# Attention and feed-forward block on one Trainium2 core: weight counting moved to the feed-forward, copies of the large products moved to ScalarE, side work held back at a unit's end

## Chip, core and metric

The kernel runs on one NeuronCore of a Trainium2 chip. The metric is the device time of one execution in microseconds (us), the median of several runs. One further execution was taken by the hardware profiler; all durations of single instructions below come from that one.

The engines go by these names: PE is TensorE's matrix multiply and PEld its weight load, DVE is VectorE, ACT is ScalarE, POOL is GpSimd, SP is SyncE, which here only issues transfers. [...]

## The reference

A transformer block in float32 for 4 sequences of 1024 tokens of 256 numbers, with 16 heads of 16 numbers, and a gated feed-forward network with 1024 hidden numbers and ternary weights:

```python
# x: (4, 1024, 256)
x = x + layernorm(attention(layernorm(x), Wqkv, Wout))
x = x + layernorm(ffn(layernorm(x), w1, w2, h1, h2, w3))

def attention(x, Wqkv, Wout):              # per head
    e = exp(clip(scores - max, -50, 50))
    attn = e / (sum(e) + 1e-6)             # out = (attn @ v) @ Wout.T

def ffn(x, ...):
    h = silu(x @ w1.T * w1_s) * (x @ w2.T * w2_s)
    h = gelu(h @ h1.T * h1_s)
    h = gelu(h @ h2.T * h2_s)
    return h @ w3.T * w3_s
```

## The kernel before

`tile_fast` computes the whole block under two assumptions: the scores are small enough to do without subtracting the maximum, and the feed-forward weights are exactly representable in the reduced type fp32r, so that one rounded copy of each weight does for an exact product. Both are tested on the chip. A column of the tile `misses` receives, for each piece of weight, the number of entries at which the weight and its rounded copy differ; two further columns per sequence tell of the scores. `judge` sums them, the sum goes into `bad`, and where `bad` is above zero `tile_general` computes all again. It isn't entered here.

**Attention.** A unit is one sequence `b`, one group `g` of 4 heads and one half `h` of the queries; there are 4 x 4 x 2 = 32 units. Each unit has 8 key chunks `c` and 2 head pairs `u`, so 16 tiles, 512 in all. For each tile `exponentials` issues 2 matmuls of scores `s` (L461) and one Exp activation `e<-s` of 128 x 1024 (L462) on ACT; `weigh` issues 4 matmuls per tile that add `e` times the values into `acc` (L469). The scores lie in the three PSUM buffers `ps`, the exponentials in a ring of 8 tiles, and `acc` has one buffer. `rise` keeps a running maximum `top` of the exponentials on DVE (L478). At the end of a unit `unit_end` copies `acc` to `o` on DVE (L275), and `divide` transposes `top` and `o` on PE into a `ps` buffer `po` (L488, L490) and divides on DVE.

**Side work.** All else is cut into small steps and put into chains of the class `Side`: the normalization of the next sequence (`gather`, `root`, `apply`), its transposes `pt`, its projections `p` (to q and k, `project`) and `pv` (to v, `values`), the ending of a finished half (transposes `po` at L516, output projection `py`, normalization, residual), the checks of the scores, and the rounding and counting of the weights. The main loop runs in turns. In a turn it issues 3 tiles of scores and exponentials, weighs 2 or 4 tiles, and calls `side.take()`, which runs the steps that are due: each step has a gap, the number of turns since the step before it in its chain, and at most one step of a turn uses PE. Side products on PE all use one PSUM buffer, `misc`; it comes free when the copy out of it has read it. The copies are made by one of two helpers:

```python
def to_scalar(o, i, scale=1.0):
    nc.scalar.activation(o, i, AF.Copy, scale=scale)
def to_vector(o, i, scale=1.0):
    nc.vector.tensor_scalar(o, i, scale, None, ALU.mult)
```

In the start-up of sequence 0 (`alone`) the copies run on ACT; later ones run on DVE (L275), except those of the last ending, which run on ACT (L272). `project` needs the product twice: `hi` is the copy in fp32r, and `lo`, made on DVE (L335), the product less `hi`.

**Weights.** `check_weights` treats 22 blocks of 128 x 1024 in one chain: a transfer on POOL's queue loads a block into `w` (L248, one buffer), POOL casts it into `wr` (L252, one buffer), DVE compares in two halves of 128 x 512 (`count`, L258, 44 in all), and after the second half POOL's queue writes `wr` to device memory (L260). Near the end of attention SP's queue loads these rounded weights into buffers that attention no longer needs.

**Feed-forward.** 8 units of 512 tokens. `gated` computes the gated layer into `ha` in 8 steps of 8 matmuls `pg` (L749), with Silu (L763) and a cast (L753) on ACT and two operations on DVE (L765, L754). `gelu_layer` runs twice, in 4 steps of 2 x 16 matmuls `ph` (L749), with Gelu on ACT (L785), a cast and a subtraction on DVE (L786, L787). `finish` computes `pz` (L802). `gated` calls `side.take()` 4 times in a unit (8 times in unit 0), each `gelu_layer` 16 times, and `side.flush()` runs what is left ahead of `finish`. The side work here is the normalization before (`prepare`) and after (`finish`) and the output stores on SP's queue.

Of the kernel before, what the change touches and what calls it, by code (L numbers as in the profile page):

```python
# [9 lines left out]
F32 = mybir.dt.float32  # L10
# [4 lines left out]
ALU = mybir.AluOpType  # L15
# [3 lines left out]
P = 128  # L19
# [16 lines left out]
NQ = 512  # L36
WIDE = 1024
# [78 lines left out]
def tile_fast(ctx: ExitStack, tc: tile.TileContext, x, wqk, wv, wo, w1, w1s, w2, w2s, h1, h1s, h2, h2s, w3, w3s, out, bad):  # L116
    nc = tc.nc
    B, S, D = x.shape
    HID = w1.shape[1]
    DC = D // P  # L120
    HC = HID // P
    NT = S // P
# [10 lines left out]
    xs = [xpool.tile([P, NT, D], F32, tag=f"x{b}", name=f"x{b}") for b in range(B)]  # L133
# [26 lines left out]
    weights = {"w1": w1, "w2": w2, "w3": w3, "h1": h1, "h2": h2}  # L160
    rows_at_once = {n: WIDE // w.shape[1] for n, w in weights.items()}
    blocks = [(n, c) for n, w in weights.items() for c in range(0, w.shape[0] // P, rows_at_once[n])]
    counts = len(blocks) * (WIDE // NQ)
    misses = const.tile([P, counts + B * 2], F32, name="misses")
    nc.vector.memset(misses, 0.0)
    rounded = {n: dram.tile(list(w.shape), F32R, name=f"{n}_r") for n, w in weights.items()}
# [11 lines left out]
    with ExitStack() as actx, ExitStack() as rctx:  # L178
# [56 lines left out]
        def misc(name):  # L235
            return ps_misc.tile([P, NQ], F32, tag="misc", name=name)

        def check_weights(n, c):

            k = blocks.index((n, c))  # L240
            st = {}

            def rows(w):
                return w[c * P : (c + rows_at_once[n]) * P, :].rearrange("(i p) d -> p i d", p=P)

            def load():
                st["w"] = work.tile([P, WIDE], F32, tag="w", name="w", bufs=1)
                nc.gpsimd.dma_start(out=st["w"].rearrange("p (i d) -> p i d", i=rows_at_once[n]), in_=rows(weights[n]))  # L248

            def cast():  # L250
                st["r"] = work.tile([P, WIDE], F32R, tag="wr", name="wr", bufs=1)
                nc.gpsimd.tensor_copy(st["r"], st["w"])  # L252

            def count(j):
                def run():
                    w, r = (t[:, NQ * j : NQ * (j + 1)] for t in (st["w"], st["r"]))
                    i = k * (WIDE // NQ) + j
                    nc.vector.scalar_tensor_tensor(w, w, 1.0, r.bitcast(F32), ALU.mult, ALU.not_equal, accum_out=misses[:, i : i + 1])  # L258
                    if NQ * (j + 1) == WIDE:
                        nc.gpsimd.dma_start(out=rows(rounded[n]).bitcast(F32), in_=st["r"].bitcast(F32).rearrange("p (i d) -> p i d", i=rows_at_once[n]))  # L260

                return run

            return [Step(load, 0, False), Step(cast, 3, False)] + [Step(count(j), 1, False) for j in range(WIDE // NQ)]

        def by_slots(o, w, i, **flags):

# [3 lines left out]
        def to_scalar(o, i, scale=1.0):  # L271
            nc.scalar.activation(o, i, AF.Copy, scale=scale)  # L272
# [4 lines left out]
        def prologue(b, space, copy):  # L277
# [38 lines left out]
            def values(t0):  # L316
                def run():
                    pv = space(f"pv_{b}_{t0}").rearrange("p (t d) -> p t d", d=D)
                    for i in range(2):
                        for c in range(DC):  # L320
                            by_slots(pv[:, i, :], st["xT"][:, c, (t0 + i) * P : (t0 + i + 1) * P], wv_sb[:, c, :], start=c == 0, stop=c == DC - 1)
                    copy(cv[:, t0 : t0 + 2, :], pv)

                return run

            def project(w, m, h):
                def run():
                    pp = space(f"p{w}_{b}_{m}_{h}")
                    for c in range(DC):
                        heads = wqk_sb[:, c, w, HPT * m : HPT * (m + 1), :].rearrange("p h d -> p (h d)")  # L330
                        by_slots(pp, heads, st["xT"][:, c, h * NQ : (h + 1) * NQ], start=c == 0, stop=c == DC - 1)
                    hi, lo = (cq[w, m, k][:, h * NQ : (h + 1) * NQ] for k in ("hi", "lo"))
                    scale = 1.0 if w else 1.0 / math.sqrt(DH)
                    copy(hi, pp, scale)
                    nc.vector.scalar_tensor_tensor(lo, pp, scale, hi.bitcast(F32), ALU.mult, ALU.subtract)  # L335

                return run
# [167 lines left out]
        def ending(b, h, copy):  # L505

            st = {}

            def transposes(c):
                def run():  # L510
                    if c == 0:
                        st["oT"] = work.tile([P, DC, NQ], F32, tag="oT", name=f"oT_{b}_{h}", bufs=1)
                        st["y"] = (both if h else work).tile([P, TPQ, D], F32, tag="y", name=f"y_{b}_{h}", bufs=1)
                    pt = misc(f"po_{b}_{h}_{c}")
                    for t in range(TPQ):
                        nc.tensor.transpose(pt[:, t * P : (t + 1) * P], on[h][:, t, c * P : (c + 1) * P], ident)  # L516
                    copy(st["oT"][:, c, :], pt)

                return run

            def project(t0):
                def run():
                    py = misc(f"py_{b}_{h}_{t0}").rearrange("p (t d) -> p t d", d=D)
                    for i in range(2):
                        for c in range(DC):
                            by_slots(py[:, i, :], st["oT"][:, c, (t0 + i) * P : (t0 + i + 1) * P], wo_sb[:, c, :], start=c == 0, stop=c == DC - 1)
                    copy(st["y"][:, t0 : t0 + 2, :], py)

                return run

            def gather(i):
                def run():
                    st["mv"] = norms.gather([st["y"][:, j, :] for j in range(i, i + 2)], i, st.get("mv"))

                return run

            def root():
                st["ln"] = norms.root(st["mv"])

            def apply(i0):  # L540
                def run():
                    for i in range(i0, i0 + 2):
                        norms.apply(st["y"][:, i, :], st["y"][:, i, :], st["ln"], i)

                return run

            def residual(i):
                def run():
                    xr = xs[b][:, h * TPQ + i : h * TPQ + i + 2, :]
                    nc.vector.tensor_add(xr, xr, st["y"][:, i : i + 2, :])  # L550

                return run

            return (
                [Step(transposes(c), 1) for c in range(DC)] + [Step(project(t), 2 if t else 1, heavy=True) for t in range(0, TPQ, 2)]
                + ([Step(open_ffn, 0, False)] if (b, h) == (B - 1, NH - 1) else [])
                + [Step(gather(i), 1, False) for i in range(0, TPQ, 2)] + [Step(root, 0, False)]
                + [Step(apply(i), 1, False) for i in range(0, TPQ, 2)] + [Step(residual(i), 1, False) for i in range(0, TPQ, 2)]
            )

        class Side:
# [27 lines left out]
                        steps.pop(0)  # L589
                return False  # L590

            def take(self):

                self.slot += 1
                self.borrowed = False
                free, heavy = True, False
                for chain in self.first + self.rest:
                    while step := self.due(chain, self.slot, free):
                        chain[0].pop(0)
                        chain[1] = self.slot  # L600
                        step.run()
                        free = free and not step.tensor
                        heavy = heavy or step.heavy
                self.tired = heavy
# [184 lines left out]
        def finish(n, i):  # L789
# [47 lines left out]
                + [Step(apply(i), 1, False) for i in range(0, TPQ, 2)] + [Step(add(t), 1, False) for t in range(0, TPQ, 2)] + [Step(store, 0, False)]  # L837
            )

        def judge():  # L840

            st = {}

            def add():
                st["total"] = small.tile([P, 1], F32, tag="total", name="total")
                nc.vector.tensor_reduce(st["total"], misses, AX.X, ALU.add)

            def run():
                pn = misc("pn")
                nc.tensor.matmul(pn[0:1, 0:1], st["total"], ones, start=True, stop=True)  # L850
                nc.vector.tensor_copy(bad, pn[0:1, 0:1])

            return [Step(add, 0, False), Step(run, 4)]

        def feed_forward():

            chain = ends[B - 1, NH - 1]
            for n in range(len(halves_of)):

                gated(ffn["a"], 2 if n else 1)  # L860
                if n + 1 < len(halves_of):
                    chain[0].extend(prepare(n + 1, to_scalar))
                if n == 1:
                    side.add(judge())
                gelu_layer(ffn["b"], ffn["a"], "h1")
                gelu_layer(ffn["a"], ffn["b"], "h2")
                side.flush()
                chain = side.add(finish(n, ffn["a"]), True)
            side.flush()
# [36 lines left out]
        early = [v[1], Step(slots(0, 0, 0, NT // 2), 0, False)]  # L906
        side.add(early + v[2:] + [Step(slots(0, 0), 0, False), Step(slots(0, 1), 0, False)] + sum(qk[1], []) + [Step(lambda: later.update(qk1=0, v=0), 0, False), Step(lambda: side.add(flags[0] + flags[1]), 0, False)])
        begin(0)
        side.add([s for k in blocks for s in check_weights(*k)])
        made = seen = weighed = 0  # L910

        def make(end):
# [6 lines left out]
        while weighed < len(tiles):  # L919
# [20 lines left out]
                        break  # L940
            make(end)
            if weighed < len(tiles):
                side.take()

        load_weights("h1", range(HC // 2, HC))
        rctx.close()
# [238 lines left out]
```

## Time and profile before

| | |
|---|---|
| median of 3 runs | 1327.92 us (1327.89 to 1328.0) |
| profiled execution, own time | 1327.01 us |
| its span | 1324.8 us |
| mean granted TensorE clock | 0.993 |
| attention with its start-up | about 0 to 650 us of the span |
| feed-forward | about 650 to 1324.8 us |
| instructions: PE, DVE, ACT, POOL | 8194, 1573, 847, 166 |

The span is the time from the first to the last instruction of the profiled execution; the 2.2 us by which its own time is longer lie around it. The busy share of an engine over the span mixes the two stages, which have different limits, so the stages are read apart. Matmul ends are modelled in the trace[...]; time in which PE waits is read from the list of waits and from the chain of work that ended last.

### The profile page before, as it was taken

To read this page: it belongs to the slowest core of one execution; us is meant where nothing else is said; L and a number is where in the kernel's file an instruction comes from. 1 tells how busy PE (TensorE), PEld (TensorE's weight loads), DVE (VectorE), ACT (ScalarE), POOL (GpSimd) and SP (SyncE) were. 2 spreads that over 40 slices of the span, in tenths; PEclk is the share of its full clock that TensorE was granted. 3 is DMA by queue.
4 is the path that set the end of the run, shared out by engine and by line. 5 is a ranking of instruction groups with operands and counts; after the bars stand their busy time and mean duration, and the time that the engine had idled before them with its cause. 6 is when DMAs were issued, how large, how long until landed. Compare 5 with 4: busy or idle time off the path is not lost.

```text
span 1324.8 us, 21087 instructions
## 1 busy us (share of the span) xinstructions
PE 1263.9 (95%) x8194; PEld 776.6 (59%) x8194; DVE 729.9 (55%) x1573; ACT 697.5 (53%) x847; POOL 119.6 (9%) x166
## 2 busy tenths in 40 slices
PE   7889998999989999989999999999999999999995
PEld 3333333333333334333578888888888888888885
DVE  3576668766696556646573543636436263463533
ACT  3688876887778878988631422414123141231410
POOL 6211112111121000000000000000000000000000
PEclk8999999999999999999999999999999999999998
DMA  4675443554444333334220000000000000000000
GB/s 130 154 188 123 107 103 97 122 116 118 104 99 118 75 65 65 56 64 167 81 112 0 1 16 1 17 0 11 6 1 17 0 17 1 0 17 0 17 0 20
DMA packets 38670, 79.76 MB, mean 60 GB/s; under 512 B 11296, under 2 KB 21152, under 8 KB 38560
## 3 DMA queue, kind: packets, MB, share of 16 engines
q1 hardware_dynamic: 30672, 53.66, 18.5%
q0 software_dynamic: 7360, 24.12, 5.6%
q8 instruction: 67, 1.10, 0.4%
q10 hardware_dynamic: 528, 0.52, 0.2%
q14 instruction: 43, 0.35, 0.1%
HBM read 28.98 MB, written 15.73 MB: 34 GB/s over the span
## 4 chain that ended last, share of the span: by engine, by line
PE 78%; DVE 11%; ACT 5%; issue 2%; DMA 2%; SPq 1%; POOL 0%; ACTq 0%; POOLq 0%; DVEq 0%
PE ph L749 35%; PE acc L469 13%; PE s L461 9%; PE pg L749 5%; PE pz L802 4%; ACT e L462 4%; PE p L269 4%; PE py L269 2%; PE pv L269 2%; DVE top L478 2%; DVE sg L765 1%; PE po L490 1%; DVE st L94 1%; DVE o L275 1%; DVE ha_lo L754 1%
## 5 line engine op out<-in xcount | busy, mean ns | idle before, releaser
L462 ACT ACTIVATE e<-s 128x1024 f32<-128x1024 f32 x512 | 485.5, 1032 | 121.2 <-PE s L461 107.3
L469 PE MATMUL acc<-e,vaug 128*32 128x512 f32 x2048 | 255.1, 600 | 1.6 <-POOL vaug L439 1.6
L785 ACT ACTIVATE a<-ph,h_scale 128x512 f32<-128x512 f32 x128 | 81.0, 685 | 306.2 <-PE ph L749 306.2
L461 PE MATMUL s<-sq,sk 64*128 64x512 f32 x1024 | 192.3, 450 | 13.9 <-ACT e L462 11.4
L749 PE MATMUL ph<-hb_lo,h 128*128 128x512 f32 x512 | 199.4, 389 | 0.0
L749 PE MATMUL ph<-hb_hi,h 128*128 128x512 f32 x512 | 199.4, 389 | 0.0
L461 PEld LDWEIGHTS s<-sq,sk 64*128 64x128 f32 x1024 | 86.0, 185 | 153.4 <-ACT e L462 119.8
L478 DVE TENSOR_TENSOR top<-top,e 128x512 f32<-128x512 f32 x192 | 135.6, 706 | 29.6 <-ACT e L462 23.4
L786 DVE CAST ha_hi<-a 128x512 fp32r<-128x512 f32 x64 | 27.1, 424 | 158.2 <-ACT a L785 158.2
L469 PEld LDWEIGHTS acc<-e,vaug 128*32 128x32 f32 x2048 | 49.2, 108 | 107.0 <-issue 98.0
L104 POOL TENSOR_TENSOR rstd<-ve,minus_half 128x4 f32<-128x4 f32 (+1 forms) x33 | 37.1, 1125 | 799.0 <-DVE ve L102 799.0
L749 PEld LDWEIGHTS ph<-hb_lo,h 128*128 128x128 f32 x512 | 96.1, 188 | 20.1
L749 PEld LDWEIGHTS ph<-hb_hi,h 128*128 128x128 f32 x512 | 96.1, 188 | 20.1
L749 PE MATMUL ph<-ha_hi,sq 128*128 128x512 f32 x256 | 101.9, 398 | 0.4
L749 PE MATMUL ph<-ha_lo,sq 128*128 128x512 f32 x256 | 99.8, 390 | 0.0
L749 PE MATMUL ph<-ha_lo,sk 128*128 128x512 f32 x256 | 99.7, 390 | 0.0
L749 PE MATMUL ph<-ha_hi,sk 128*128 128x512 f32 x256 | 99.7, 389 | 0.0
L765 DVE SCALAR_TENSOR_TENSOR sg<-pg,w_scale,sg 128x512 f32<-128x512 f32 x64 | 47.1, 745 | 48.1 <-ACT sg L763 48.1
L763 ACT ACTIVATE sg<-pg,w_scale 128x512 f32<-128x512 f32 x64 | 43.3, 688 | 55.1 <-DVE ha_lo L754 44.3
L786 DVE CAST hb_hi<-a 128x512 fp32r<-128x512 f32 x64 | 27.0, 422 | 80.4 <-ACT a L785 80.4
L269 PE MATMUL p<-xT,wqk_sb 128*32 128x512 f32 x512 | 61.6, 602 | 2.0 <-DVE xT L275 1.1
L749 PEld LDWEIGHTS ph<-ha_hi,sq 128*128 128x128 f32 x256 | 48.3, 189 | 12.8 <-DVE sg L765 3.4
(145 smaller groups left out, 1649.7 us busy)
## 6 DMA issues: line engine op xcount, KB each, us to landing
w<-in_h_dram POOLq DMA_DIRECT2D x16, 512.0 KB, 4.7
h_r<-wr POOLq DMA_DIRECT2D x16, 512.0 KB, 3.4
sk<-ck1hi SPq DMA_DIRECT2D x64, 64.0 KB, 2.3
sk<-ck1lo SPq DMA_DIRECT2D x64, 64.0 KB, 2.3
sq<-cq1hi SPq DMA_DIRECT2D x64, 64.0 KB, 2.3
sq<-cq1lo SPq DMA_DIRECT2D x64, 64.0 KB, 2.3
h<-h_r SPq DMA_DIRECT2D x8, 512.0 KB, 6.4
sk<-ck0hi SPq DMA_DIRECT2D x56, 64.0 KB, 2.3
```

The source lines that it names most:

```text
L104: nc.gpsimd.tensor_tensor(rstd[:, :n], ve[:, :n], self.minus_half[:, :n], ALU.pow)
L269: nc.tensor.matmul(o[j : j + SLOT, :], w[:, j : j + SLOT], i, **flags)
L461: nc.tensor.matmul(s[:, a, :], stacks[1, g % 2, u][r, c * P : (c + 1) * P], stacks[0, g % 2, u][r, h * NQ : (h + 1) * NQ], start=True, sto ...
L462: nc.scalar.activation(pair(k)[:, u], s, AF.Exp)
L469: nc.tensor.matmul(acc[SLOT * i : SLOT * (i + 1), :], vaug[g % 2][:, c, i, :], pair(k)[:, i // 2, i % 2, :], start=c == 0, stop=c == NT - 1)
L478: nc.vector.tensor_max(top, top if c > 1 else pair(k - 2)[:, :, :, 0:P], pair(k)[:, :, :, 0:P])
L749: nc.tensor.matmul(p, homes[n][c][:, m * P : (m + 1) * P], half[:, c, :], start=c == 0 and k == 0, stop=c == len(homes[n]) - 1 and k == 1)
L763: nc.scalar.activation(sg, p[:, 0, :], AF.Silu, scale=scales["w1"][:, m : m + 1])
L765: nc.vector.scalar_tensor_tensor(sg, p[:, 1, :], scales["w2"][:, m : m + 1], sg, ALU.mult, ALU.mult)
L785: nc.scalar.activation(a, p[:, j, :], AF.Gelu, scale=scales[n][:, m : m + 1])
L786: nc.vector.tensor_copy(o[0][:, m, :], a)
L802: nc.tensor.matmul(p[t], half[:, c, t * P : (t + 1) * P], homes["w3"][c], start=c == 0 and k == 0, stop=c == HC - 1 and k == 1)
```

## The change

Three edits.

- Rounding and counting are parted. In attention `round_weights` loads, casts and writes each block with no step on DVE. In the feed-forward a new `check_weights` makes 44 pieces of 128 x 512. For each, SP's queue loads the weight again into one of two slots in the buffer of sequence 0 (`xs[0]`, whose first half is free from unit 2 on), and DVE compares it with the rounded copy that lies in on-chip memory. Units 2 to 6 take 9, 9, 9, 9 and 8 pieces, queued after `gated` and ahead of the two `gelu_layer`s; `judge` follows in unit 6 instead of unit 1.
- `values`, `project` and, except for the last sequence, the output projection `py` copy their products with `to_scalar` wherever they run. `xT`, `oT` and `o` stay on DVE, and so do the subtractions for `lo`.
- `Side.take` has a flag `calm`. With it set, steps that don't use PE wait for a later turn. It is set when no more than 4 tiles of the current unit are left to weigh (or no more than are made and not yet weighed, if that is fewer).

```diff
-    counts = len(blocks) * (WIDE // NQ)
+    counts = sum(w.shape[0] * w.shape[1] for w in weights.values()) // (P * NQ)
...
-        def check_weights(n, c):
-            k = blocks.index((n, c))
+        def round_weights(n, c):
...
             def cast():
                 st["r"] = work.tile([P, WIDE], F32R, tag="wr", name="wr", bufs=1)
                 nc.gpsimd.tensor_copy(st["r"], st["w"])
-            def count(j):
-                def run():
-                    w, r = (t[:, NQ * j : NQ * (j + 1)] for t in (st["w"], st["r"]))
-                    i = k * (WIDE // NQ) + j
-                    nc.vector.scalar_tensor_tensor(w, w, 1.0, r.bitcast(F32), ALU.mult, ALU.not_equal, accum_out=misses[:, i : i + 1])
-                    if NQ * (j + 1) == WIDE:
-                        nc.gpsimd.dma_start(out=rows(rounded[n]).bitcast(F32), in_=...)
-                return run
-            return [Step(load, 0, False), Step(cast, 3, False)] + [Step(count(j), 1, False) for j in range(WIDE // NQ)]
+                nc.gpsimd.dma_start(out=rows(rounded[n]).bitcast(F32), in_=...)
+            return [Step(load, 1, False), Step(cast, 3, False)]
...
-                    copy(cv[:, t0 : t0 + 2, :], pv)
+                    to_scalar(cv[:, t0 : t0 + 2, :], pv)
...
-                    copy(hi, pp, scale)
+                    to_scalar(hi, pp, scale)
                     nc.vector.scalar_tensor_tensor(lo, pp, scale, hi.bitcast(F32), ALU.mult, ALU.subtract)
...
-                    copy(st["y"][:, t0 : t0 + 2, :], py)
+                    (copy if b == B - 1 else to_scalar)(st["y"][:, t0 : t0 + 2, :], py)
...
-            def take(self):
+            def take(self, calm=False):
...
-                    while step := self.due(chain, self.slot, free):
+                    while (step := self.due(chain, self.slot, free)) and (step.tensor or not calm):
...
+        def check_weights():
+            parts = []
+            for n, w in weights.items():
...
+                        parts.append(count(len(parts), w[...].rearrange("(i p) d -> p i d", p=P), n, c, j))
+            return parts
+        def count(k, rows, n, c, j):
+            st = {}
+            def load():
+                st["w"] = xs[0][:, 2 * (k % 2) : 2 * (k % 2) + 2, :].rearrange("p t d -> p (t d)")
+                nc.sync.dma_start(out=st["w"].rearrange("p (i d) -> p i d", i=rows.shape[1]), in_=rows)
+            def run():
+                r = spare[6 + c // (HC // 2)][:, D * c % WIDE :][:, :NQ] if n == "w3" else homes[n][c][:, j : j + NQ]
+                nc.vector.scalar_tensor_tensor(st["w"], st["w"], 1.0, r.bitcast(F32), ALU.mult, ALU.not_equal, accum_out=misses[:, k : k + 1])
+            return [Step(load, 1, False), Step(run, 2, False)]
...
             for n in range(len(halves_of)):
                 gated(ffn["a"], 2 if n else 1)
...
-                if n == 1:
-                    side.add(judge())
+                if 1 < n < len(halves_of) - 1:
+                    size = -(-len(checks) // (len(halves_of) - 3))
+                    side.add(sum(checks[size * (n - 2) : size * (n - 1)], []) + (judge() if n == len(halves_of) - 2 else []))
...
-        side.add([s for k in blocks for s in check_weights(*k)])
+        side.add([s for k in blocks for s in round_weights(*k)])
...
-                side.take()
+                left = 2 * (NT - tiles[weighed][3])
+                side.take(left <= min(4, made - weighed))
```

More of the change, by code (lines that the diff above doesn't have):

```diff
@@ L252, in cast @@
                 nc.gpsimd.tensor_copy(st["r"], st["w"])
-            def count(j):
-                def run():
-                    w, r = (t[:, NQ * j : NQ * (j + 1)] for t in (st["w"], st["r"]))
-                    i = k * (WIDE // NQ) + j
-                    nc.vector.scalar_tensor_tensor(w, w, 1.0, r.bitcast(F32), ALU.mult, ALU.not_equal, accum_out=misses[:, i : i + 1])
-                    if NQ * (j + 1) == WIDE:
-                        nc.gpsimd.dma_start(out=rows(rounded[n]).bitcast(F32), in_=st["r"].bitcast(F32).rearrange("p (i d) -> p i d", i=rows_at_once[n]))
-                return run
-            return [Step(load, 0, False), Step(cast, 3, False)] + [Step(count(j), 1, False) for j in range(WIDE // NQ)]
+                nc.gpsimd.dma_start(out=rows(rounded[n]).bitcast(F32), in_=st["r"].bitcast(F32).rearrange("p (i d) -> p i d", i=rows_at_once[n]))
+            return [Step(load, 1, False), Step(cast, 3, False)]
         def by_slots(o, w, i, **flags):
@@ L838, in finish @@
             )
+        def check_weights():
+            parts = []
+            for n, w in weights.items():
+                inner = min(w.shape[1], NQ)
+                i = NQ // inner
+                for c in range(0, w.shape[0] // P, i):
+                    for j in range(0, w.shape[1], inner):
+                        parts.append(count(len(parts), w[c * P : (c + i) * P, j : j + inner].rearrange("(i p) d -> p i d", p=P), n, c, j))
+            return parts
[8 more added lines that the diff above has]
+            return [Step(load, 1, False), Step(run, 2, False)]
         def judge():
@@ L857, in feed_forward @@
             chain = ends[B - 1, NH - 1]
+            checks = check_weights()
             for n in range(len(halves_of)):
```

## The prediction

> **What bounds the kernel now.** I read the page first (busy shares, the 40 slices, the chain that ended last), then busy time by stretch, then PE's waits, then the chain inside a crowded stretch.
>
> ```profile
> PE 1263.9 (95%) x8194; PEld 776.6 (59%) x8194; DVE 729.9 (55%) x1573; ACT 697.5 (53%) x847; POOL 119.6 (9%) x166
> ...
> DVE  3576668766696556646573543636436263463533
> ACT  3688876887778878988631422414123141231410
> ...
> PE 78%; DVE 11%; ACT 5%; issue 2%; DMA 2%; SPq 1%; POOL 0%; ACTq 0%; POOLq 0%; DVEq 0%
> ```
>
> The whole-span shares hide two stages. In attention (slices 1 to 20) ACT stands at 8 tenths and DVE at 6 to 7, with a 9 for DVE in one slice; in the feed-forward both are half idle or more. PE carries 78% of the chain, so only the other 22% can be won.
>
> ```profile
> 40.00:540.00 500.00, 471.69 (x3999) 177.08 (x3991) 340.92 (x729) 396.22 (x435) 75.38 (x98) 1.00 0.47 106
> 200.00:250.00 50.00, 44.43 (x360) 16.49 (x362) 44.19 (x107) 34.72 (x39) 11.35 (x14) 0.97 0.50 117
> 340.00:410.00 70.00, 63.67 (x560) 24.80 (x550) 57.89 (x139) 54.83 (x60) 15.56 (x18) 1.00 0.49 116
> 540.00:650.00 110.00, 100.32 (x724) 36.49 (x723) 58.92 (x124) 97.01 (x103) 3.61 (x4) 1.00 0.39 95
> 650.00:1324.80 674.80, 661.00 (x3241) 550.11 (x3239) 317.41 (x683) 187.66 (x289) 19.17 (x18) 0.99 0.04 15
> ```
>
> The columns after the length are PE, PEld, DVE, ACT, POOL busy us. At 200:250 and 340:410 DVE is busy 88% and 83% of the time: there DVE sets the pace. At 540:650, the last sequence, which has next to no side work, it is ACT (88%). In the feed-forward PE is at 98% and DVE at 47%.
>
> ```profile
> PE po L488 <- DVE top L478: 9.7, 8, 2.2
> PE s L461 <- ACT e L462: 3.2, 10, 0.7
> PE py L269 <- DVE oT L275: 2.7, 2, 2.0
> PE po L490 <- DVE o L275: 2.5, 11, 0.2
> PE pt L311 <- DVE bounds L393: 1.9, 1, 1.9
> ```
>
> These are the longest matmul waits of 40:540 (us, times, longest). With the four smaller DVE lines (1.6, 1.2, 1.1, 1.1) PE waits 21.8 us for DVE. The largest is at a unit's end: `po` can't start because DVE hasn't got to `top`.
>
> ```profile
> 393.05 0.61 DVE w L258 x2
> 393.66 0.60 DVE xT L275
> 394.26 0.61 DVE top L478
> 394.96 0.70 DVE top L478
> 395.80 0.63 PE po L488 x4
> ```
>
> This is the chain ahead of such a wait: a count (`w`, L258) and a copy stand in DVE's queue before the `top` that PE waits for. Neither is urgent.
>
> [...]
> - [...] the chain above walks through DVE instructions that have nothing to do with `po`.
> - [...] The trace has 597 to 601 ns for such copies (L272); I use 0.60 us.
> - [...] its table loads stand at L763 and L785 alone, 8 each, though copies stand between the Gelus.
>
> ```profile
> L258 DVE SCALAR_TENSOR_TENSOR w<-w,wr 128x512 f32<-128x512 f32 x44 | 30.0, 683 | 0.0
> L275 DVE TENSOR_SCALAR cv<-pv 128x512 f32<-128x512 f32 x15 | 10.4, 691 | 30.0 <-PE pv L269 30.0
> L272 ACT ACTIVATE cq0hi<-fpt 128x512 fp32r<-128x512 f32 x14 | 8.4, 599 | 43.2 <-PE fpt L738 43.2
> ```
>
> **The change part by part.**
>
> *Counting leaves attention.* 44 x 0.683 = 30.0 us go from DVE (and 44 accumulator reads of 0.08). POOL's 22 loads no longer wait for DVE's counts (169.8 us of POOL waits, on no path of weight) and a block takes 4 turns instead of 5, so rounding ends at about turn 88 instead of 110. The same 22 loads (4.7 us to landing) and 22 writes (3.4 us) run somewhat denser, at a DMA share of 0.5, beside the stacking copies on SP's queue; later loads of rounded weights find them ready sooner. Cost 0.
>
> *Copies move to ACT.* Counting the copies in both instruction streams, 55 change engine: 15 `cv`, 28 `hi`, 12 `y`. DVE loses 55 x 0.69 = 38.0 us; ACT gains 55 x 0.60 = 33 us. With the counts, DVE falls from 341 to some 273 us of these 500, and by a fifth in the crowded stretches. ACT rises from 396 to 429.
>
> The new wait: the copy stands in ACT's queue ahead of the next Exps and waits for the side product. Who waits behind it: up to three Exps, through them the `ps` buffers and the next scores; for `hi`, also `lo` on DVE, and `misc` comes free only after `lo`. Cover: ACT's own idle time ahead of Exps, 91.5 us in 40:540. At 162.9 to 169.5 us one sees how: six Exps take 5.65 us, then ACT idles 1.0 us until the scores behind the product `p` arrive. `p` ends about 0.5 us before those scores, so a copy of 0.60 us ends about when the first Exp could start: 0.0 to 0.15 us late. If the cover is gone (the same cycle also holds squares of 0.64 us), it costs its full 0.60. I take 0.07 on average, 55 x 0.07 = 4 us; bounds 0 and 33.
>
> *Calm turns.* In the last one or two turns of each of the 32 units DVE gets nothing but `top`, `lo` and `o`. That is aimed at the 9.7 us. What was held comes in the turn after, so some of it is late there: the transposes `pt`, `po` and `py` that wait for normalization or `oT`. PE's stream keeps its length; some 60 rows of it change place, side products a turn or so later.
>
> *What is won in attention.* Of the 9.7 us I let 7.5 go (DVE keeps 2 or 3 `top`s of 0.7 us to do there). Of the 9.6 us of waits for `oT`, `bounds`, `cq1lo`, `norm`, `xT`, I let 6.5 go: the queue ahead of them shortens by a fifth, and the copies that stood among them are gone. The 2.5 us for `o` stay: that copy has to follow `acc`. Exps wait 4.4 us for `top` to free ring buffers; 1 us of it reaches PE. Sum: -15 us. Next late: the scores that wait for ACT. The stretch 540:650 has no moved copy and no count and stays.
>
> *Counting in the feed-forward.* 44 x 0.68 = 30 us for DVE, 9 per unit of 82 us: DVE goes from 47% to 55%. They are queued behind `gated`, and 9 x 3 turns fit in the 32 turns of the two Gelu layers, away from `gated`, where DVE runs late (PEld waits 5.9 us there in all 8 units). In the Gelu layers a count can hold a split up by at most 0.77 us; three `ps` buffers and the order of the chunks (the next layer needs the last two only after some 5 us) hide it. If that cover were gone: 44 x 0.68 = 30 us. I take +1. 44 loads of 256 KB on SP's queue (one such load landed in 2.7 us) get two turns, 3.6 us, and mostly more, since a load waits only for the count two before it. The output stores share that queue, issue 0.36 us each, and from unit 3 on stand ahead of the loads. `judge` moves 5 units later, and still ends a unit before `bad` is read. Cost 0.
>
> Sum: -15 + 4 + 1 = **-10 us** on the profiled execution's own 1327.0, giving 1317. The median of the runs is 0.9 above that execution, so **1318**.
>
> **The rivals.**
> - *ACT becomes the bound (slower).* The copies meet Exps that have no gap. Place: turns that carry a copy and two squares, or a short turn (0.89 + 1.0 us of PE with a 1.73 us product: 3.6 us, against 3 Exps, 2.8, and a copy, 0.6). It decides as soon as a copy costs more than 0.27 us on average, since 55 x 0.27 = 15 eats the gain. At the full 0.60: 33 - 15 + 1 = +19, so 1347; at 0.4, +8, so 1336. Against it: 91.5 us of ACT waiting for PE. For it: at 540:650, at 88%, ACT does set the pace, and after the change 40:540 stands at 86%. Chance 0.12.
> - *The relief changes nothing.* Held steps bunch after the unit's end and the same PE steps wait there; or PE's waits for DVE are only changed into waits for ACT. Then -1 to +1 with the copies' small price: 1327. For it: 471.7 of 500 us of PE are busy already. Chance 0.10.
> - *More is won.* PE work in 40:540 by its undisturbed pace (s 0.149, acc 0.116, p 0.108, pv and py 0.054 us each) leaves some 40 us of gaps, twice the listed waits. If the Exps' rhythm recovers too, 25 us go: 1303. Included in the forecast's side as its far end.
>
> **How the numbers follow.** Forecast -2.7 us or better: 0.78. Within 0.2% (2.7 us, about what a measurement of this kernel can tell from no change): 0.10. Slower beyond it: 0.12. The range goes from the far end, 1303, to 1330, which takes in no change; left out are most of the ACT cases (0.12) and some 0.06 below.
>
> **What would show it.** After: DVE at some 55% in 40:540, no L258 rows before the feed-forward, PE's wait of `po` for `top` at 3 us or less, attention some 11 us shorter, units of the feed-forward still 82 us. Wrong if PE or PEld waits for ACT grow by over 15 us, if Exps start late behind `cv`, `hi`, `y`, or if `ph` waits for DVE in units 2 to 6.

## The result, and the profile after

The changed kernel takes **1323.53 us** (median of 6 runs, 1322.06 to 1326.24); the kernel before took 1328.70 us in 6 runs (1327.89 to 1331.75). The ratio is 0.9959, with a 95% interval of 0.9944 to 0.9973: faster by some 5 us, about half of what was forecast. The profiled execution took 1322.63 us (span 1320.8), 4.4 us less than the one before.

The page after: the busy line, ACT's forty slices, the shares of the chain that ended last.

```profile
PE 1267.2 (96%) x8194; PEld 777.2 (59%) x8194; DVE 696.2 (53%) x1518; ACT 724.1 (55%) x902; POOL 119.1 (9%) x166
...
ACT  4788887888888888898631412314223142231410
...
PE 76%; DVE 10%; ACT 9%; issue 3%; POOL 1%; DMA 1%; SPq 0%; ACTq 0%; POOLq 0%; DVEq 0%
```

DVE has 55 copies less (1573 to 1518 instructions) and ACT 55 more (847 to 902). The copies brought no table load: ACT's stand where they stood before, 8 at each of the feed-forward's two lines (L753 and L775 here, L763 and L785 before) and one in the start-up (L156), of 1.28 us each. In the chain, ACT has grown from 5% to 9% and DVE shrunk by a single per cent. Busy time by stretch after (PE, PEld, DVE, ACT, POOL behind the length, then the granted clock):

```profile
40.00:540.00 500.00, 478.76 (x4034) 180.06 (x4030) 287.41 (x607) 428.45 (x494) 75.93 (x99) 1.00 0.47 106
340.00:410.00 70.00, 66.82 (x560) 25.78 (x560) 49.73 (x124) 60.94 (x70) 12.57 (x15) 1.00 0.46 99
```

DVE has fallen from 341 to 287 us of the 500, and in the crowded stretch 340:410 from 83% to 71%; ACT stands there at 87% now. The longest waits of PE in 40:540 after (total us, times, longest). The diff shifts line numbers: scores are L451 (L461 before), `po` L478 and L480 (L488, L490).

```profile
PE s L451 <- ACT e L452: 7.3, 21, 0.7
PE po L480 <- DVE o L265: 3.9, 17, 0.2
PE py L259 <- DVE oT L265: 2.1, 2, 1.7
...
PE po L478 <- DVE top L468: 0.8, 3, 0.3
```

The wait of `po` for `top` is gone, from 9.7 to 0.8 us. All of PE's waits for DVE fell from 21.8 to 11.7 us; those for ACT rose from 4.7 to 7.3, a net of 7.5 us. The first matmul of the feed-forward starts at 642.48 us, before at 649.46, so 7.0 earlier. That the two figures are so close is in part chance: the profiled run before also lost 3.4 us more to dips of PE's clock (last section). The feed-forward gives 3.0 of it back: it takes 678.3 us instead of 675.3 (span less that start).

ACT's own waits in the same stretch, after:

```profile
ACT e L452 <- PE s L451: 31.8, 37, 1.5
ACT y L262 <- PE py L259: 9.2, 11, 2.2
ACT cv L262 <- PE pv L259: 7.9, 12, 1.1
...
ACT cq1hi L262 <- PE p L259: 4.2, 7, 1.1
```

Before, the Exps waited longer for their scores:

```profile
ACT e L462 <- PE s L461: 91.5, 90, 3.6
```

Now ACT spends 29.8 us waiting for the products that it has to copy (the three lines here and three shorter ones of `hi`). The cover that the forecast counted on is largely used up.

### The profile page after: what moved, and what is told of

Same layout as the page of the kernel before. It is cut to its first block, busy times and chain, and to the rows that moved or that the text cites. A ratio compares the mean times of both kernels' runs of the same rounds, so it can differ in the third digit from the quotient of the medians.

```text
span 1320.8 us, 21125 instructions
## 1 busy us (share of the span) xinstructions
PE 1267.2 (96%) x8194; PEld 777.2 (59%) x8194; DVE 696.2 (53%) x1518; ACT 724.1 (55%) x902; POOL 119.1 (9%) x166
## 4 chain that ended last, share of the span: by engine, by line
PE 76%; DVE 10%; ACT 9%; issue 3%; POOL 1%; DMA 1%; SPq 0%; ACTq 0%; POOLq 0%; DVEq 0%
PE ph L739 35%; PE acc L459 12%; PE s L451 8%; ACT e L452 7%; PE pg L739 5%; PE pz L792 4%; PE p L259 4%; PE py L259 2%; PE pv L259 2%; DVE top L468 2%; PE po L480 1%; DVE sg L755 1%; DVE o L265 1%; DVE st L94 1%; DVE ha_lo L744 1%
## 5 line engine op out<-in xcount | busy, mean ns | idle before, releaser
L775 ACT ACTIVATE a<-ph,h_scale 128x512 f32<-128x512 f32 x128 | 81.1, 686 | 306.6 <-PE ph L739 306.6
L451 PE MATMUL s<-sq,sk 64*128 64x512 f32 x1024 | 193.2, 449 | 17.6 <-ACT e L452 15.0
L451 PEld LDWEIGHTS s<-sq,sk 64*128 64x128 f32 x1024 | 86.2, 184 | 158.3 <-ACT e L452 125.8
L753 ACT ACTIVATE sg<-pg,w_scale 128x512 f32<-128x512 f32 x64 | 43.3, 688 | 55.0 <-DVE ha_lo L744 43.1
L739 PEld LDWEIGHTS ph<-ha_hi,sq 128*128 128x128 f32 x256 | 48.4, 189 | 12.7 <-DVE sg L755 3.3
```

Of the source, the lines that this page charges most:

```text
L451: nc.tensor.matmul(s[:, a, :], stacks[1, g % 2, u][r, c * P : (c + 1) * P], stacks[0, g % 2, u][r, h * NQ : (h + 1) * NQ], start=True, sto ...
L739: nc.tensor.matmul(p, homes[n][c][:, m * P : (m + 1) * P], half[:, c, :], start=c == 0 and k == 0, stop=c == len(homes[n]) - 1 and k == 1)
L753: nc.scalar.activation(sg, p[:, 0, :], AF.Silu, scale=scales["w1"][:, m : m + 1])
L775: nc.scalar.activation(a, p[:, j, :], AF.Gelu, scale=scales[n][:, m : m + 1])
```

## The experiments

Each kernel ran in five rounds beside runs of the kernel before on the same chip. Medians are set against those; "at like clock" compares runs whose mean granted TensorE clock is the same, because runs of one kernel differ by it (last section): the kernel before takes 1327.2 to 1327.7 us at 0.994 and 1330.8 to 1331.9 at 0.988. Such a comparison leaves out what a change does by way of the clock; the medians keep it.

| kernel | median us | ratio to before (95%) | runs at 0.994, mean us | first feed-forward matmul at |
|---|---|---|---|---|
| after | 1323.53 | 0.9959 (0.9944 to 0.9973) | 1323.0 (3 runs) | 642.48 |
| **a_counts** | 1319.97 | 0.9931 (0.9918 to 0.9945) | 1319.7 (3) | 640.00 |
| **b_copies** | 1329.95 | 1.0007 (0.9998 to 1.0016) | none | 652.97 |
| **c_calm** | 1323.39 | 0.9959 (0.9945 to 0.9973) | 1321.7 (1) | 644.97 |
| **late** | 1320.43 | 0.9936 (0.9923 to 0.9950) | 1320.3 (4) | 643.55 |
| **ac** | 1322.00 | 0.9942 (0.9928 to 0.9956) | 1320.4 (2) | 642.23 |
| **ac_spin** | 1322.73 | 0.9953 (0.9939 to 0.9967) | none | 642.10 |
| **ac_hi** | 1320.18 | 0.9935 (0.9922 to 0.9949) | 1320.1 (3) | 643.68 |
| **ac_late** | 1319.83 | 0.9927 (0.9913 to 0.9940) | 1317.9 (1) | 643.58 |
| **a_late** | 1317.57 | 0.9912 (0.9898 to 0.9926) | 1317.4 (4) | 639.98 |
| **ac_hi_late** | 1318.36 | 0.9917 (0.9903 to 0.9932) | none | 640.86 |
| **ac_cvy** | 1321.60 | 0.9942 (0.9928 to 0.9956) | 1321.8 (3) | 641.64 |
| **ab** | 1322.22 | 0.9947 (0.9934 to 0.9961) | 1321.8 (3) | 642.31 |

The letters: a is the move of the counting, b the copies on ACT, c the holding back. The kernel before had medians of 1328.53 (19 runs), 1328.83 (9) and 1328.55 (11) in the three batches. Each batch ran on another chip, so a comparison across batches rests on these three medians being alike.

### Each part alone

**a_counts** is the changed kernel with the other two edits undone:

```diff
-                    to_scalar(cv[:, t0 : t0 + 2, :], pv)
+                    copy(cv[:, t0 : t0 + 2, :], pv)
-                    to_scalar(hi, pp, scale)
+                    copy(hi, pp, scale)
-                    (copy if b == B - 1 else to_scalar)(st["y"][:, t0 : t0 + 2, :], py)
+                    copy(st["y"][:, t0 : t0 + 2, :], py)
-                side.take(left <= min(4, made - weighed))
+                side.take()
```

> Only the counting is moved; copies and side work as before. Theory (queue theory: PE waits because DVE's queue is crowded, so any work taken out of it helps): DVE loses 30 us in attention, the first feed-forward matmul starts 3 to 5 us earlier than the 649.5 us of before, and the feed-forward loses the 3 us that it lost with the whole change; in all 0 to 2 us faster. Rival (placement theory: only the wait of po for top at a unit's end counts, and average load is harmless): attention gains under 1.5 us, so in all 1.5 to 3 us slower than before.

Moving the counts alone gives 1319.97 us. It wins 8.6 us, more than the whole change and more than the theory and its rival had expected. PE's waits for DVE in 40:540 fall from 21.8 to 14.4 us: `po` for `top` only from 9.7 to 6.8, but the waits for `oT`, `bounds`, `norm`, `xT`, `cq1lo` from 9.6 to 4.9. Two that are left:

```profile
PE po L478 <- DVE top L468: 6.8, 8, 1.8
...
PE py L259 <- DVE oT L265: 1.7, 1, 1.7
```

Attention ends 9.5 us earlier in the profile. All of PE's listed waits, those for ACT and POOL included, fall by 6.1 us, and clock dips take 1.7 us less; the rest is not located. The edit also lets POOL load and cast the weights faster one after another: the last of the 22 casts begins at 392.8 us in the changed kernel, which has the same edit, and at 432.9 before. No run separates that from the counts, but PE's waits for POOL are 1.1 us in both kernels, and no wait of PE for a transfer is listed in either.

**b_copies** is the kernel before with the three copy edits:

```diff
-                    copy(cv[:, t0 : t0 + 2, :], pv)
+                    to_scalar(cv[:, t0 : t0 + 2, :], pv)
-                    copy(hi, pp, scale)
+                    to_scalar(hi, pp, scale)
-                    copy(st["y"][:, t0 : t0 + 2, :], py)
+                    (copy if b == B - 1 else to_scalar)(st["y"][:, t0 : t0 + 2, :], py)
```

> Only the copies go to ScalarE; counting stays in attention, no calm turns. Queue theory: DVE loses 38 us, attention gains 4 to 6 us less some 3 us of ACT delays, so 1 to 3 us faster than before, feed-forward unchanged at 675.3 us. Rival (ACT-bound theory: the copies' delays of the Exps are what ate the expected gain): attention is no faster or slower than before, and the waits of PE and PEld for ACT e grow by over 10 us.

The interval, 0.9998 to 1.0016, allows no gain worth the name, though DVE's busy time in 40:540 falls by 35 us. PE's waits for DVE fall by 1.9 us only and those for ACT rise by 1.2. The wait that the relief was to end is nearly all there:

```profile
PE po L488 <- DVE top L478: 8.1, 6, 2.1
```

So the theory missed. The rival was right that nothing is won, but the waits for ACT by which it was to be known did not grow by 10 us: those of the weight loads fell, from 114.1 to 110.4 us.

**c_calm** is the kernel before with the holding back:

```diff
-            def take(self):
+            def take(self, calm=False):
...
-                    while step := self.due(chain, self.slot, free):
+                    while (step := self.due(chain, self.slot, free)) and (step.tensor or not calm):
...
-                side.take()
+                left = 2 * (NT - tiles[weighed][3])
+                side.take(left <= min(4, made - weighed))
```

> Only the calm turns; counting and copies stay on DVE in attention. Queue theory: the wait of po for top (9.7 us) falls to 3 us or less, but the held steps come later behind a queue that is as full as before, so half of it returns: 2 to 4 us faster. Placement theory: the whole 6 to 8 us show. Rival (bunching): the held steps make pt, py and p late by as much as was won: within 1 us of before.

It gives 5.1 us, between the two theories. PE's waits in 40:540 of this kernel show a rival of the prediction at work in part: held steps are late next.

```profile
PE pt L311 <- DVE norm L367: 1.8, 1, 1.8
...
PE pv L269 <- DVE bounds L393: 1.2, 1, 1.2
PE po L488 <- DVE top L478: 1.2, 4, 0.3
PE p L269 <- DVE norm L367: 1.2, 1, 1.2
```

`po` waits 1.2 us for `top` instead of 9.7, but the waits for `norm`, `bounds` and their like rise from 9.6 to 12.5, and those for `o` from 2.5 to 3.9.

### The feed-forward's 3 us

**late** is the whole change with the counts of a unit starting ten turns later, and one turn less between a load and its count:

```diff
-            return [Step(load, 1, False), Step(run, 2, False)]
+            return [Step(load, 1, False), Step(run, 1, False)]
...
-                    side.add(sum(checks[size * (n - 2) : size * (n - 1)], []) + (judge() if n == len(halves_of) - 2 else []))
+                    side.add([Step(lambda: None, 10, False)] + sum(checks[size * (n - 2) : size * (n - 1)], []) + (judge() if n == len(halves_of) - 2 else []))
```

> The whole change, with the 9 counts of a feed-forward unit started 10 turns later, and run 1 turn after their load instead of 2, so that none stands ahead of the next unit's normalization. Theory: the 3.0 us that the feed-forward lost are one count of 0.61 us in each of units 2 to 6 ahead of the normalization that the transposes fpt wait for; then the first gelu layer goes back from 30.75 to 30.15 us in units 2 to 6, and the whole is 3 us faster than the changed kernel, at 0.9935 of before. Rival (the loads' traffic or DVE's load as such): the layers stay at 30.75 us.

In the trace the loss sits in the first Gelu layer of units 2 to 6, the units with counts: 30.74 to 30.79 us each after, 30.14 to 30.17 before. The cause is DVE's queue. Its timeline after, in unit 2 (start, length):

```profile
837.27 0.18 DVE L95 BATCH_NORM_AGGREGATE mv<-st 128x2 f32<-128x6 f32 x1
837.37 0.68 DVE L851 SCALAR_TENSOR_TENSOR x<-x,ck0hi 128x512 f32<-128x512 f32 x1
837.97 0.08 DVE L851 DVE_READ_ACCUMULATOR x<-x,ck0hi 128x1 f32 x1
837.97 0.42 DVE L94 BATCH_NORM_STATS2 st<-x 128x6 f32<-128x256 f32 x1
```

The first count (L851) stands in the middle of the next unit's normalization. The normalized tokens `fxn` begin 12.34 us into the layer instead of 11.71, and the transposes `fpt` on PE trickle behind them. The chain of waits, first after, then before:

```profile
842.04 1.10 PE fpt L728 x4
843.15 1.85 PE ph L739 x8
```

```profile
849.69 0.47 PE fpt L738 x4
850.16 1.86 PE ph L749 x8
```

Four transposes hold PE for 1.10 us instead of 0.47 here. The layers show the same 0.6 us in each of the five units, 3.0 us together. With the later start the layers of **late** are back at 30.11 to 30.15 us and the median at 1320.43, as the theory had it.

### Whether the parts add up

**ac** keeps counting and holding back; the copies stay on DVE (the first three pairs of lines of a_counts).

> The whole change without the copies on ScalarE: counting moved and calm turns, the 55 copies on DVE as before. The single edits moved the first feed-forward matmul by -9.5 us (counting), -4.5 us (calm) and +3.5 us (copies), the whole change by -7.0. ACT-cost theory (the copies' cost on ACT's queue is what ate the expected gain): attention is 3 to 5 us shorter than with the whole change, first feed-forward matmul at 637.5 to 639.5 us, 0.9915 to 0.993 of before. Rival (overlap theory: counting and calm turns win the same waits of po for top, and the copies cost little once DVE is free): attention stays within 1 us of the whole change's 642.5.

At like clock it takes 1320.4 us, no less than the counting alone (1319.7). The parts do not add: a gives 8.6 us by its median, c 5.1, both 6.8. PE's waits say part of why. With both, `po` waits 1.2 us for `top`, as with c, but the other waits for DVE, without `o`, are back at 8.6 us from 4.9, and those for `o` at 3.7 from 2.7. Of the 5.6 us that the holding back wins at the unit's end it gives back 4.7, most of it at the next transposes. With ACT's part the list still puts ac 2.3 us ahead of a_counts, and the times don't show it. Why is open; two clock dips behind the start-up, 3.5 us together, stand in ac's profile and none in that of a_counts.

**ac_late** is ac with the later start of **late**.

> Counting moved and calm turns, copies on DVE, and the counts started 10 turns later in each feed-forward unit. Theory: the gains add, since they lie in different stages: 3.0 us below the first of this list, some 0.989 to 0.991 of before, the fastest so far. Rival: the feed-forward's 3 us return but attention's gain without the copies isn't there: equal to the earlier run with later counts, 0.9936.

It takes 1319.83 us, 2.2 below ac by the medians, with overlapping intervals, and lies between theory and rival.

**ab** has counting and copies, nothing held back (the last pair of lines of a_counts).

> The counting and the copies together, with nothing held back. Theory (the copies win nothing that the counting has not won, and cost 2 to 3 us on ScalarE): 1322 to 1323 us, ratio 0.9955. Rival (the copies on ScalarE add a gain of their own once the counts are gone): 1319 us or less, ratio 0.9925 or less.

1322.22 us: as the theory had it. By the medians the copies make the counting alone 2.2 us slower. The intervals of the two ratios overlap, but every one of the six runs (1321.07 to 1324.26) is slower than every one of the five of a_counts (1319.11 to 1320.6).

### What the copies cost on ACT, and why

Pairs that differ in the copies alone are ab against a_counts, after against ac, late against ac_late, and b_copies against before. At like clock the copies cost 2.2, 2.6 and 2.4 us at 0.994, and 1.3 us at 0.992 (1329.3 in 6 runs against 1328.0 in 2). Some of these stand on one or two runs (the table has their numbers), the one run of b_copies at 0.993 is 0.4 us below the kernel before, and no pair's ratios are apart by their intervals; but these four have one sign, and so have the differences of the medians (2.2, 1.5, 0.6 and 1.4 us).

The chain of waits after shows the form of the loss:

```profile
399.48 1.76 PE p L259 x16
...
401.26 0.42 ACT cq0hi L262
...
401.77 0.38 ACT e L452
...
402.66 1.96 ACT e L452 x2
```

Between the product `p` and the next Exps stands its copy, which could not begin before `p` ended (at 401.24 us; the copy begins at 401.26). The chain reaches the Exp behind it through the copy, not through its scores.

**ac_spin** tells mere occupancy of ACT from this waiting: on top of ac, with the copies on DVE, ACT makes 55 copies of 128 x 512 from on-chip memory onto itself, at the same places, which wait for no product.

```diff
+        def turn_scalar(t):
+            z = xs[t][:, TPQ + 2 : TPQ + 4, :]
+            nc.scalar.activation(z, z, AF.Copy)
...
                     copy(hi, pp, scale)
+                    if not alone:
+                        turn_scalar(3 if b in (1, 2) else 0)
```

(and likewise behind `cv` and `y`)

> As the kernel before this one in the list, the copies on DVE, and at the place in ACT's queue where each moved copy would stand, a copy of a 128x512 tile of on-chip memory onto itself, which waits for no product; it is extra work and leaves the result as it is. Occupancy theory: what costs is 0.6 us of ACT's time ahead of Exps; attention is as long as with the whole change (first feed-forward matmul 641.5 to 643.5 us). Rival (head-of-line theory: what costs is ACT waiting for the side product, and lo on DVE waiting for ACT): attention is within 1 us of the kernel without copies on ACT.

ACT's busy time in 40:540 rises from 404 to 429 us, as in the changed kernel, and the first feed-forward matmul starts at 642.10 us, in ac at 642.23. The two profiles carry the same clock dips, 6.8 and 6.9 us, so 25 us more of busy ACT cost attention nothing there. That start alone doesn't part theory and rival, though, since the changed kernel's own, 642.48, lies as near with dips of 1.7 us only. The runs lean to the rival: at 0.991 and 0.993 ac_spin takes 0.7 and 0.6 us more than ac, the changed kernel 3.1 and 2.0 (one or two runs each). The intervals of all three ratios overlap. That the waiting costs, and not the occupancy, is thus likely and not settled.

**ac_hi** puts only the 28 `hi` copies on ACT, **ac_cvy** only the 27 copies of `cv` and `y`; each takes its lines from the changed kernel and the others from ac.

> As the first of this list, with only the 28 hi copies of the projections on ScalarE; cv and y stay on DVE. If each moved copy costs the same, about half of what the 55 cost. Head-of-line theory: more than half, since lo on DVE waits for hi, and misc comes free after both. Occupancy theory: half or less, since these copies fall where PE has 1.73 us of product to do and ACT idles.

> The counting and the holding back, with only the cv and y copies on ScalarE; the hi copies stay on VectorE. Theory (the cv and y copies carry the cost, since ScalarE's next Exp stands behind a copy that waits for a product that ends late): 1322.5 to 1323 us, ratio 0.995. Rival (the copies cost by their number, wherever they are, or nothing): 1320 to 1321.5 us.

ac_hi, 1320.18 us, is level with ac at 0.994 (1320.1 against 1320.4); its single runs at 0.993 and 0.991 are 0.4 and 1.1 us slower. ac_cvy, 1321.60 us, lies between theory and rival: its median is ac's, at 0.994 it is 1.4 us slower (1321.8, 3 runs), at 0.993 0.5 us faster (2 runs against one). The runs at 0.994 point at `cv` and `y`, whose copies also wait longest, 17.1 us for 27 where the `hi` copies wait 12.7 for 28; those at other clocks don't. Which copies cost most is not settled by these runs.

### The best version

**a_late** is a_counts with the later start of the counts; **ac_hi_late** is ac_hi with it.

> The counting alone is moved into the feed-forward, and there it begins ten turns later in each unit. Theory (the counts held up the next unit's normalization by some 0.6 us in each of five units, and starting later takes that away; the counting itself is what the attention gains from): 3 us less than the counting alone took, about 1317 us, ratio 0.991 to 0.992; first-gelu layers of the feed-forward's units 2 to 6 back at 30.1 to 30.2 us. Rival (what starting later gave the whole change lay in the attention's luck with the clock): as the counting alone, 1320 us, ratio 0.993.

> The counting and the holding back, with only the 28 copies of the large projections' hi parts on ScalarE, and the counts ten turns later. Theory (the hi copies cost nothing on ScalarE, the late counts give 3 us): about 1317 to 1318 us, ratio 0.992. Rival (any copy on ScalarE costs its share, 28 of 55 of some 2.6 us): 1319 to 1320 us.

a_late has the lowest median: 1317.57 us, as the theory had it, ratio 0.9912 (0.9898 to 0.9926), beneath the whole interval of the changed kernel. Attention ends where a_counts ends it (639.98 and 640.00 us), and the Gelu layers are back at 30.14 to 30.17. ac_hi_late, 1318.36, can't be told from it by the intervals; it lies a little above its theory.

## Why the prediction was right or wrong

The direction was right. That the median lay in the range says little, since the range took in no change. The size was half of the forecast, -5.2 us for -10, and one of the three edits, the copies, took away from what the other two won. Step by step, on the profiled executions:

- **`po` for `top`.** -7.5 forecast, -8.9 measured (9.7 to 0.8): right, and it was the holding back that did it (c_calm).
- **The other waits for DVE.** The step "Of the 9.6 us ... I let 6.5 go: the queue ahead of them shortens by a fifth" failed: 9.6 became 7.0, so -2.6. a_counts shows that the counts alone would have brought them to 4.9; held steps put most of that back. The queue is shorter, but what it holds comes in a bunch. This was named under calm turns ("some of it is late there") and given no number.
- **"The 2.5 us for `o` stay."** They became 3.9; c_calm and ac show nearly the same (3.9, 3.7), a_counts 2.7. So +1.4 came with the holding back; why was not tried.
- **Exps waiting for `top`.** 4.4 us became 5.2; the 1 us did not come.
- **Copies on ACT, +4.** PE's waits for ACT rose by 2.6 us, so the 0.07 us per copy was measured at 0.05; cover and place were read rightly. What was wrong is that the relief of DVE by these 38 us was part of the -15: b_copies shows that it brings no more than it costs. The prediction had read from DVE's 88% and 83% that "there DVE sets the pace". But b_copies takes 35 us from its busy time in 40:540 and wins nothing, and a_counts takes 18 and wins most, so the total does not decide. That single steps in the wrong order do, as in the chain that the prediction shows, fits all runs; step by step it was not tried.
- **Feed-forward, +1.** +3.0 measured. The step that failed is the cover, "three `ps` buffers and the order of the chunks": the splits were covered, but the counts also stood ahead of the next unit's normalization, which the step did not name; `late` takes the loss away. The sign set for it in advance, `ph` waiting for DVE, came as `fpt` waiting for `fxn`: the weight loads of `fpt` waited 2.2 us in 12 waits instead of 0.4 in 2.

Together: -8.9 - 2.6 + 1.4 + 2.6 = -7.5 in attention's listed waits, against -11 forecast, and +3.0 for +1. That -7.5 came out near the 7.0 us of attention owes something to luck, since the clock dips, which the sum leaves out, took 3.4 us less. The signs: DVE in 40:540 stands at 57% (55 forecast), attention is 7.0 us shorter (11), feed-forward units with counts take 82.4 us (82; the last of them, with `judge`, 82.7). The weight loads' waits for ACT in 40:540, a sign of being wrong, did not grow (114.1 before, 112.5 after). Of the rivals, "the relief changes nothing" came true of the copies alone. ACT as the bound did not come, but its first stage did: the chain's ACT share rose from 5 to 9%. "More is won" was out of reach of these three edits together; counting alone, started later, gets 11 us by its median.

Two readings of the prediction are a little off, with no effect on the sum. One more table load stands in the start-up, at L156. And the landing times of 4.7 and 3.4 us are those of 16 of the 22 blocks; the other 6 took 5.6 and 3.7.

One thing stays open. Between ac and the changed kernel PE's listed waits for ACT and DVE grow by 0.9 us (+2.7 and -1.8), where the time at like clock grows by 2.6; the rest was not located.

## What to carry to other kernels

Take an engine's low-priority work out of the crowded stage before moving its urgent work elsewhere: moving the counts, for which POOL's next loads waited (169.8 us in 40:540 before) and no matmul in the list of waits, was worth more here than all three edits together (8.6 us by the medians against 5.2). Edits that shorten the same queue can win the same waits (here 8.6 and 5.1 us alone, 6.8 together), so price them together, once, and run each alone. Work moved into a stage where the engine is half idle (DVE was busy 47% of the feed-forward before) still has to be put behind the few instructions there that PE waits for; ten turns of delay were worth 2 to 3 us.

## What was not expected of the hardware

After the start-up, the profiled attention has one dip of the granted clock before and two in ac. Each stands in or right behind a stretch in which PE was partly idle: before at 208 to 216 us, behind 4 us with PE busy for 2.43; in ac at 228 to 236 us, behind 4 us with PE busy for 2.54, and at 380 to 388 us, where PE was busy for 2.12 of the first 4. Three stretches of 4 us before, the clock in the third column from the end:

```profile
204.00:208.00 4.00, 2.43 (x18) 0.94 (x18) 3.79 (x12) 2.69 (x4) 2.87 (x4) 1.00 0.82 200
208.00:212.00 4.00, 3.58 (x36) 1.92 (x38) 3.33 (x10) 0.37 (x2) 0.00 (x0) 0.67 0.61 186
212.00:216.00 4.00, 3.81 (x28) 1.33 (x26) 3.71 (x9) 2.84 (x3) 2.38 (x3) 0.91 0.00 0
```

and the first two of them after:

```profile
204.00:208.00 4.00, 3.23 (x46) 1.60 (x50) 3.69 (x9) 1.79 (x3) 0.59 (x1) 1.00 0.79 212
208.00:212.00 4.00, 3.77 (x36) 1.53 (x28) 2.31 (x7) 2.67 (x4) 0.00 (x0) 1.00 0.02 5
```

PE was busy 2.43 of 4 us, and the clock fell to 0.67 and 0.91: 4 x 0.33 + 4 x 0.09 = 1.7 us of full clock lost. Each of ac's two dips lost as much (0.66 and 0.91; 0.86 and 0.71). After, PE was busy 3.23 us there and kept its clock. But a low busy share is not enough by itself: before, 224:228 had PE busy for 2.45 us and 388:392 for 2.12, and no dip followed. Nor is a long wait: the dip at 208 us came behind a wait of 2.0 us (`py` for `oT`), while none followed the longest listed wait of 40:540, 2.2 us of `po` for `top`, which ended at 57 us. What sets a dip off is not shown. By stretches of 10 us, the profiled attention lost 5.1 us to dips before, 1.7 after, 3.4 in a_counts and 6.9 in ac; of this 3.4, 1.7, 3.4 and 3.4 us lie in the first 40 us, the start-up. That is why profiled starts of the feed-forward compare kernels only to within a few us (ac's 642.23 and ac_cvy's 641.64 carry 6.9 and 3.4 us of it), and it may be why the medians of ac and ac_cvy are alike though ac is faster at 0.994. The mean clock of all runs listed here is 0.991 for the kernel before (39 runs) and 0.993 for a_counts and after (5 and 6). If it is idle stretches that bring the dips, a wait that PE no longer has can be worth more than its length, by an estimate from these dips up to 1.7 us more; no run tests that by itself.
